# Layer 2 of a four-layer graph network on one Trainium2 core: counts in array quarters, ordered through POOL, and evicted by column chunk

## The chip, the core and the metric

The kernel runs on one core of a Trainium2 chip. The core has five engines that each take their own queue in order[...]: PE (TensorE, matrix products, with its weight loads shown apart as PEld), DVE (VectorE), ACT (ScalarE), POOL (GpSimd) and SP (which issues the DMAs here).[...] The metric is the device time of one execution in microseconds. The kernel before takes 688.06 us (median of 3 runs, 685.46 to 690.53).

## What is computed

Four graph layers follow each other on 3327 nodes with 64 features and one dense 3327 x 3327 adjacency matrix, each with a layer norm and a residual. The change concerns the third of them, which is called layer 2 in the code:

```python
support = input @ weight
mask = (adj != 0).astype(support.dtype)
rank = jnp.cumsum(mask, axis=1)
deg = rank[:, -1:]
k = jnp.minimum(deg, float(MAX_NEIGH))        # MAX_NEIGH = 100
pos = rank - (deg - k)
w = mask * jnp.where(pos > 0, DECAY ** (k - pos), 0.0)   # DECAY = 0.5
out = w @ support + bias
```

A neighbour's weight is a power of one half whose exponent is the number of neighbours that come after it in the row. So what is needed of every entry of the adjacency is a count: how many entries of its row further on are not zero.

## The kernel before

**Tiles.** The nodes are padded to 26 blocks of 128. The targets (the rows of the adjacency) are split in two groups, `GROUPS[0]` with 768 and `GROUPS[1]` with 896 targets in each of two halves h. A group's columns are cut in two chunks, `g.chunks`: 384 and 384 columns in group 0, 384 and 512 in group 1. I call group 1, which comes first, wide and group 0 narrow.

**Blocks.** `work` lists 52 pieces of work (i, c, a): group i, source chunk c from 12 down to 0, and a = 1 and then 0. Piece n covers 128 sources; two pieces, a = 1 and a = 0, make a pair and share two masks. `mask(n + 2)` makes the mask of the piece two further on: DVE compares an adjacency tile that SP's queue has loaded with zero and writes bf16. `stream` plans the loads.

**Counts.** `count(n, h)` (line 1657) multiplies masks by constant 128 x 64 triangles. The result of half h lies in `cnt[h]`, a PSUM tile of two banks; there counts go on accumulating from piece to piece, so each eviction reads a running total. Two source blocks s give the lower and the upper 64 partitions of the result, so that two matmuls with 64 weight columns each use the two halves of the array side by side. In the a = 1 pieces `rest_a` has its content in rows 0 to 63 and zeros in the other rows, and `tri_b` has its content in rows 64 to 127 and zeros in the others; both are applied with all 128 rows. `tri_a`, in the a = 0 pieces, fills all rows.

**Evictions.** `S.activation(w, e, AF.Relu, bias=ebias)` (line 1669) turns counts into 16-bit patterns that are read again as bf16 powers of two. That is ACT's work; the last three evictions with a = 0 and h = 1 are done by DVE (line 1667).

**Products.** `weigh(n, q)` (line 1681) multiplies the support, split into the three bf16 `parts`, by the weights `ws[n]` of column chunk q: six matmuls, accumulated in `acc2`. It trails the counts: `todo` holds (n, q) that wait, and `flush(n, most)` takes one or two of them after each `count` if they are at least `LAG` = 1 piece old and if the generator that makes their support has been issued.

**Order.** Engines run in the order of issue. Between counts, `weave.tick()` lets generators issue pieces of neighbouring stages: the end of layer 1 and the support at the beginning of layer 2 (`support`, up to some 318 us), and, once the wide group is finished, the node quantities of layer 3 (`nodes3`, lines 997 to 1144). The latter also issues the `xw<-xs` transfers on POOL's queue (lines 1049 and 1050). When the wide group is done, POOL clears the `pack` and `p2c` tiles (lines 1744 and 1745); in time this happens far earlier, since POOL has nothing else to do. After the last piece DVE makes two attention products of layer 3 (line 1290), clears accumulators (line 1758) and takes the sums of group 0 (`m_t`, line 640), from which the node chain of layer 3 goes on (line 537).

`gates` (line 752), in layer 0, is named by the prediction because it uses matmuls with 64 rows and 64 columns, a quarter of the array each:

```python
r = D * ((1 - h) ^ o)
product(out, h, (w_mh, w_hm)[h][:, 2, :], slice(r, r + D))
```

Of the kernel before, what the change touches and what calls it, by code (L numbers as in the profile page):

```python
# [8 lines left out]
F32 = mybir.dt.float32  # L9
BF16 = mybir.dt.bfloat16  # L10
# [8 lines left out]
D = 64  # L19
P = 128  # L20
NB = 26
# [52 lines left out]
GROUPS = [Group(0, 6), Group(6, HB)]  # L74
# [238 lines left out]
def gnn_kernel(ctx: ExitStack, tc: tile.TileContext, t, out):  # L313
    nc = tc.nc
    V, S, G, T = nc.vector, nc.scalar, nc.gpsimd, nc.tensor
# [13 lines left out]
    p0 = ctx.enter_context(left("p0"))  # L329
# [80 lines left out]
    weave = Weave()  # L410
# [11 lines left out]
    for i in range(2):  # L422
# [18 lines left out]
    tri_b, tri_a, rest_a, ones64 = (  # L441
        p0.tile([P, D], BF16, name=n) for n in ("tri_b", "tri_a", "rest_a", "ones64")
    )
    ebias, hg, lastf = (p0.tile([P, 1], F32, name=n) for n in ("ebias", "hg", "lastf"))
    last = p0.tile([P, 1], I32, name="last")

    scrap = p0.tile([P, 1], F32, name="scrap")
    pick = p0.tile([P, 8, 2], F32, name="pick")
    halves = p0.tile([P, 2], F32, name="halves")
    G.iota(last, pattern=[[0, 1]], base=0, channel_multiplier=1)  # L450
# [50 lines left out]
    def pair(i):  # L501

        return ps.tile([P, 1024], F32, name="pair", tag=f"pair{i}")
# [184 lines left out]
    edges = [nd.tile([P, 2 * g.w], BF16, name="edges", tag=f"edges{g.c0}") for g in GROUPS]  # L688
# [39 lines left out]
    for i, (ca, cb) in enumerate(starts):  # L728
        g = Group(ca, cb, part=i % 2)
# [130 lines left out]
    n = len(s_src) + len(f_src)  # L860
# [10 lines left out]
    n = len(LAYER1) - len(f_src)  # L871
# [12 lines left out]
    parts = [mb16[:, i * NB * D : (i + 1) * NB * D] for i in range(2)]  # L884
# [722 lines left out]
    with ExitStack() as c2:  # L1607
        mk = c2.enter_context(right("l2"))
        c2x = c2.enter_context(ExitStack())
        mkx = c2x.enter_context(right("l2x"))  # L1610
        WB, WL = 7, 3
        LAG = 1


        work = [(i, c, a) for i in (1, 0) for c in reversed(range(HB)) for a in (1, 0)]
        masks, ws, cnt, acc2, todo = {}, {}, {}, {}, []

        def mask(n):

            if n < len(work):  # L1620
                a = stream.tile(stream.now)
                w = 2 * GROUPS[work[n][0]].w
                masks[n] = (
                    spare if n == 4 else mk.tile([P, WIDE], BF16, name="mask", tag=f"mask{n % 5}")
                )
                V.tensor_scalar(masks[n][:, :w], a, 0.0, None, op0=OP.not_equal)  # L1626
                stream.done()

        def weights(n):
            b = n % (WB if n < NB else WL)  # L1630
            pool = mk if b < WL else mkx
            ws[n] = pool.tile([P, WIDE], U16, name="w", tag=f"w{b}")

        def count(n, h):

            i, c, a = work[n]
            g = GROUPS[i]
            first = n % NB == 0
            if h == 0 and n not in ws:
                weights(n)  # L1640
            if first:
                cnt[h] = pair(h)
            m = n - n % 2
            for lo, hi in g.chunks:
                cs = slice(h * g.w + lo, h * g.w + hi)
                terms = []
                if first:
                    terms.append([(ones64, edges[i][:, cs]), (tri_b, masks[m + 1][:, cs])])
                    terms.append([(tri_b, masks[m][:, cs])])
                elif a:  # L1650
                    terms.append([(rest_a, masks[m - 2 + s][:, cs]) for s in range(2)])
                    terms.append([(tri_b, masks[m + s][:, cs]) for s in range(2)])
                else:
                    terms.append([(tri_a, masks[m + s][:, cs]) for s in range(2)])
                for j, both in enumerate(terms):
                    for s, (l, r) in enumerate(both):
                        T.matmul(  # L1657
                            cnt[h][s * D : (s + 1) * D, P + lo : P + hi],
                            lhsT=l,
                            rhs=r,  # L1660
                            start=first and j == 0,
                            stop=j == len(terms) - 1 or first and s == 1,
                            skip_group_check=True,
                        )
            w, e = ws[n][:, h * g.w : (h + 1) * g.w], cnt[h][:, P : P + g.w]
            if gen_n and not weave.runs(gen_n) and a == 0 and h:
                V.tensor_scalar(w, e, ebias, 0.0, op0=OP.add, op1=OP.max)
            else:
                S.activation(w, e, AF.Relu, bias=ebias)  # L1669

        def weigh(n, q):
            i, c, a = work[n]
            g = GROUPS[i]
            if n % NB == 0 and q == 0:
                if i == 0:
                    weave.until(gen_s)
                acc2[i] = accumulators((0, 1) if i == 0 else (2, 3))
            lo, hi = g.chunks[q]
            for j, p in enumerate(parts):
                for h in range(2):  # L1680
                    T.matmul(  # L1681
                        acc2[i][q][h * D : (h + 1) * D, : hi - lo],
                        lhsT=p[:, 2 * c + a, :],
                        rhs=ws[n][:, h * g.w + lo : h * g.w + hi].bitcast(BF16),
                        start=n % NB == 0 and j == 0,
                        stop=n % NB == NB - 1 and j == 2,
                    )

        def flush(n, most):
            while todo and most and todo[0][0] <= n - LAG:  # L1690
                gens = need[work[todo[0][0]][1]]
                if weave.runs(*gens):
                    if len(todo) < 2 * WB:
                        return
                    weave.until(*gens)
                weigh(*todo.pop(0))
                most -= 1


        for n in range(WL):  # L1700
            weights(n)
        spare = mk.tile([P, WIDE], BF16, name="mask", tag="mask4")
        for n in range(2):
            mask(n)
        m_s = evicted(gs_, acc_s)
        gen_s = weave.add(support(gs_, m_s), 1, gen_f)
        need = {c: (gen_f if c >= gf.c0 else gen_s,) for c in range(HB)}
        gen_n = None
        for n in range(len(work)):
            mask(n + 2)  # L1710
            for part in range(2):
                count(n, part)
                flush(n, 2 if len(todo) > 2 * LAG + 2 else 1)
                todo.append((n, part))
                weave.tick()
            if gen_n or todo[0][0] < NB:
                continue

            m_f = evicted(gf, acc2[1], b_l2)
            turn["banks"] = (2, 3)  # L1720
            c2x.close()
            cc.close()
            stream.close(range(SLOTS2, SLOTS1))
            n3 = ctx.enter_context(left("n3"))
            h = n3.tile([P, NB, D], F32, name="h3")
            c3 = ctx.enter_context(ExitStack())
            n3f = c3.enter_context(left("n3f"))
            xd = n3f.tile([P, NB, D], F32, name="xd")

            xs = n3f.tile([P, HN], F32, name="xs")  # L1730
            xw = n3f.tile([P, HN], F32, name="xw")
            rows_j = n3f.tile([P, NP], BF16, name="rows_j")
            rows_i = n3f.tile([P, NP], BF16, name="rows_i")
            leftb = n3f.tile([P, NP], F32, name="leftb")
            p2c = n3f.tile([P, NB, 31 + ROWS], F32, name="p2c")
            x2, qs, pn, rpn, lefts, righth, B1, Bq2, alq, xq = (
                n3.tile([P, NB], F32, name=n)
                for n in "x2 qs pn rpn left righth B1 Bq2 alq xq".split()
            )
            least = n3.tile([P, 2], F32, name="least")  # L1740

            packs = [n3f.tile([P, GROUPS[1].nb, P], BF16, name=f"pack{i}") for i in range(2)]
            for a in packs:
                G.memset(a, 0.0)
            G.memset(p2c, 0.0)
            onesl = n3f.tile([12, P], BF16, name="onesl")
            V.tensor_scalar(onesl, last[:12, :].to_broadcast([12, P]), 9.0, None, op0=OP.is_ge)
            gen_n = weave.add(nodes3(gf, m_f))
            weave.add(early3(), 1, gen_n)
        flush(len(work) + LAG, len(todo))  # L1750
        while weave.running:
            weave.tick()
        for name, *args in (("attention_t", 0), ("attention_d", 0)):
            made3.add((0, name, *args))
            STEPS3[name](0, *args)
        x0, x1 = bank(2), bank(3)
        for a in (x0, x1):
            V.memset(a, 0.0)
        m_s = evicted(gs_, acc2[0], b_l2)
# [406 lines left out]
```

## Time and profile before

The profiled execution has a span of 680.8 us from its first to its last instruction; the median of the timed runs is 688.06 us.

| engine | busy us | share of the span | instructions |
|---|---|---|---|
| PE | 627.6 | 92% | 5656 |
| DVE | 457.4 | 67% | 725 |
| ACT | 391.2 | 57% | 561 |
| POOL | 9.3 | 1% | 19 |

Layer 2's own groups of instructions, from the page and from the answers by line:

| line | engine | what | count | median of one, ns |
|---|---|---|---|---|
| 1657 | PE | count matmuls `tri_b`, `tri_a`, `rest_a` | 208, 208, 192 | 326 |
| 1681 | PE | product matmuls | 624 | 326 |
| 1626 | DVE | masks | 52 | 1083 |
| 1669 | ACT | evictions | 101 | 992 |
| 1667 | DVE | evictions | 3 | 1018 |

Matmuls are pipelined, and a record also covers the way through the array: in a steady stream pairs of matmuls with 384 columns start every 0.16 us, although each record takes 0.33 us. How often the next one starts is what a matmul costs PE. The page's slices divide the span into 40 parts of 17 us; a digit is the busy share in tenths.

### The profile page before, as it was taken

The page shows a single profiled execution, that of the slowest core. Times are in us where ns is not written, and L with a number is a line of the kernel's source. Part 1 is how long each engine was busy: PE and PEld are TensorE (multiplying, and loading weights), DVE is VectorE, ACT ScalarE, POOL GpSimd, SP SyncE. Part 2 cuts the span into 40 slices and gives each one's busy share as a digit, 9 for nine tenths or more (in the row PEclk, how much of TensorE's full clock was granted, in tenths as well). Part 3 has the DMA queues.
Part 4 walks back from the last instruction along what each step waited for, and adds up shares of the span by engine and source line. Part 5 has one row for each costly group of instructions (what it writes and reads, how often), then busy time and mean ns, then how long its engine had stood idle before and what let it go on. Part 6 is the DMA issues. An engine that isn't in the chain of part 4 may idle for free.

```text
span 680.8 us, 13348 instructions
## 1 busy us (share of the span) xinstructions
PE 627.6 (92%) x5656; PEld 348.0 (51%) x5656; DVE 457.4 (67%) x725; ACT 391.2 (57%) x561; POOL 9.3 (1%) x19
## 2 busy tenths in 40 slices
PE   2988999999989999899998996799999999999993
PEld 1442444244334333466665663466666666676781
DVE  3331876544788705676558656699888889988875
ACT  3112200310354203588887788699899988988813
POOL 0000000000000000200001000100000000000000
PEclk9999999999999999999999999699999999999996
DMA  8999999099996999988787954157666666656401
GB/s 337 414 416 418 359 381 366 7 362 419 419 411 230 416 419 416 405 335 305 267 310 244 360 189 144 23 145 237 201 226 204 198 202 211 195 176 196 155 2 55
DMA packets 32531, 183.41 MB, mean 269 GB/s; under 512 B 3696, under 2 KB 4752, under 8 KB 32464
## 3 DMA queue, kind: packets, MB, share of 16 engines
q1 hardware_dynamic: 32112, 181.63, 72.2%
q0 software_dynamic: 352, 0.85, 0.5%
q8 instruction: 46, 0.75, 0.4%
q14 instruction: 21, 0.17, 0.1%
HBM read 180.76 MB, written 0.85 MB: 267 GB/s over the span
## 4 chain that ended last, share of the span: by engine, by line
PE 79%; DVE 8%; DMA 6%; ACT 5%; issue 1%; SPq 0%; DVEq 0%; ACTq 0%
PE bank L651 26%; PE bank L1330 17%; PE pair L1223 8%; PE pair L1657 7%; PE pair L1317 6%; PE bank L1681 6%; DMA adj<-in_adj 5%; PE pair L752 2%; ACT w L1669 2%; PE pair L556 1%; PE bank L1427 1%; DMA xn<-in_x 1%; PE bank L526 1%; PE bank L1057 1%; PE bank L1545 0%
## 5 line engine op out<-in xcount | busy, mean ns | idle before, releaser
L651 PE MATMUL bank<-adj,m_a 128*64 128x384 f32 (+1 forms) x832 | 153.8, 516 | 8.0 <-DMA adj<-in_adj 5.6
L651 PEld LDWEIGHTS bank<-adj,m_a 128*64 128x64 f32 x832 | 56.8, 137 | 94.6 <-issue 71.3
L1669 ACT ACTIVATE w<-pair,ebias 128x896 uint16<-128x896 f32 (+1 forms) x101 | 93.4, 954 | 17.2 <-PE pair L1657 16.0
L651 PE MATMUL bank<-adj,m_b 128*64 128x384 f32 (+1 forms) x416 | 76.7, 515 | 1.4 <-ACT hm L740 1.4
L1279 ACT ACTIVATE tr<-leftb,righth 128x256 f32<-128x256 f32 x156 | 66.4, 496 | 0.8 <-PE bank L1330 0.8
L1626 DVE TENSOR_SCALAR mask<-adj 128x1792 bf16<-128x1792 f32 (+1 forms) x52 | 52.8, 1034 | 18.8 <-PE pair L1657 18.8
L379 DVE SCALAR_TENSOR_TENSOR edges<-adj,edges 128x1792 bf16<-128x1792 f32 (+1 forms) x24 | 44.9, 1890 | 30.3 <-DMA adj<-in_adj 30.2
L1327 DVE SCALAR_TENSOR_TENSOR tr<-pair,tr 128x1024 f32<-128x1024 f32 (+3 forms) x52 | 49.7, 957 | 22.2 <-PE pair L1317 20.0
L1233 ACT ACTIVATE sq<-pair 128x1024 f32<-128x1024 f32 (+1 forms) x52 | 47.5, 912 | 22.6 <-PE pair L1223 21.7
L740 ACT ACTIVATE hm<-bank 64x384 f32<-64x384 f32 (+1 forms) x8 | 4.1, 513 | 93.1 <-DVE mh L739 92.8
L1681 PE MATMUL bank<-w,m_b 128*64 128x384 bf16 (+1 forms) x416 | 56.2, 339 | 0.0
L1223 PE MATMUL pair<-xs,xw 64*128 64x512 f32 (+3 forms) x120 | 54.7, 542 | 1.4 <-ACT sq L1233 1.4
L1223 PE MATMUL pair<-xs 64*128 64x512 f32 (+3 forms) x120 | 54.7, 542 | 1.2 <-ACT sq L1233 1.2
L1308 DVE SCALAR_TENSOR_TENSOR dir<-sq,dir 128x1792 f32<-128x1792 f32 (+2 forms) x27 | 52.5, 1946 | 0.0
L1290 DVE SCALAR_TENSOR_TENSOR dir<-dir,adj 128x1792 f32<-128x1792 f32 x26 | 52.4, 2016 | 0.0
L651 PEld LDWEIGHTS bank<-adj,m_b 128*64 128x64 f32 x416 | 29.0, 137 | 45.6 <-issue 41.9
L1256 ACT ACTIVATE dir<-leftb,righth 128x1792 f32<-128x1792 f32 (+6 forms) x38 | 48.5, 1307 | 0.0
L1243 ACT ACTIVATE sq<-sq,hg 128x1792 f32<-128x1792 f32 x26 | 46.6, 1791 | 0.8
L1317 PE MATMUL pair<-ident,sq 128*128 128x128 f32 x312 | 45.5, 282 | 0.1
L1290 DVE SCALAR_TENSOR_TENSOR tr<-tr,adj 128x1280 f32<-128x1280 f32 (+2 forms) x26 | 45.5, 1751 | 0.0
L1317 PEld LDWEIGHTS pair<-ident,sq 128*128 128x128 f32 x312 | 33.5, 142 | 22.2 <-issue 11.8
L1330 PE MATMUL bank<-dir,xd 128*64 128x384 f32 (+3 forms) x264 | 43.6, 460 | 0.0
(312 smaller groups left out, 948.2 us busy)
## 6 DMA issues: line engine op xcount, KB each, us to landing
adj<-in_adj SPq DMA_DIRECT2D x108, 896.0 KB, 6.3
adj<-in_adj SPq DMA_DIRECT2D x92, 768.0 KB, 8.2
adj<-in_adj SPq DMA_DIRECT2D x12, 640.0 KB, 4.0
xn<-in_x SPq DMA_DIRECT2D x3, 192.0 KB, 5.4
out<-w SPq DMA_DIRECT2D x3, 192.0 KB, 2.4
xw<-xs POOLq DMA_DIRECT2D x4, 128.0 KB, 4.0
w_l<-in_w_l SPq DMA_DIRECT2D x1, 460.0 KB, 9.8
xn<-in_x SPq DMA_DIRECT2D x1, 256.0 KB, 7.1
```

Of the source, the lines that this page charges most:

```text
L651: T.matmul(acc[q][h * D : (h + 1) * D, : hi - lo], lhsT=m[:, k, :], rhs=a[:, h * g.w + lo : h * g.w + hi], start=first, stop=last,)
L1223: T.matmul(p[:, o : o + n], lhsT=l, rhs=r, start=not rows, stop=rows)
L1256: S.activation(columns(dirs[m, b], ph.n)[:, :, first * P : first * P + n], left_of(ph.g)[:, :, o : o + n], AF.Tanh, bias=righth[:, 2 * c + ...
L1279: S.activation(a[:, e * 2 * P : (e + 1) * 2 * P].rearrange("p (b c) -> p b c", b=2), left_of(ph.s)[:, :, o : o + P], AF.Tanh, bias=righth[ ...
L1290: V.scalar_tensor_tensor(a[:, :w], a[:, :w], 1.0, stream.tile(stream.now), op0=OP.add, op1=OP.mult)
L1308: V.scalar_tensor_tensor(a[:, :, cs], s[:, :, cs], HD, a[:, :, cs], op0=OP.add, op1=OP.mult)
L1317: T.transpose(p[:, o : o + P], columns(sqs[m, b], PHASES[m].n)[:, k, i * P : (i + 1) * P], ident,)
L1327: V.scalar_tensor_tensor(a, pts.pop((m, k, "t"))[:, :n], HD, a, op0=OP.add, op1=OP.mult)
L1330: T.matmul(out, lhsT=lhsT, rhs=rhs, start=False, stop=True, skip_group_check=True)
L1626: V.tensor_scalar(masks[n][:, :w], a, 0.0, None, op0=OP.not_equal)
L1669: S.activation(w, e, AF.Relu, bias=ebias)
L1681: T.matmul(acc2[i][q][h * D : (h + 1) * D, : hi - lo], lhsT=p[:, 2 * c + a, :], rhs=ws[n][:, h * g.w + lo : h * g.w + hi].bitcast(BF16), s ...
```

## The change

`count` now takes a column chunk q in place of a half h, so `cnt[q]` holds both halves of one chunk, one in each bank, and `evict` reads 2 x 384 or 2 x 512 columns. Products are queued in pieces of two matmuls, (n, q, j) for the part j, and `flush`'s limits are three times as high. In a = 1 pieces that are not the first of their group, and for which a product piece can be issued, the counts are made by `count_rows` with matmuls of 64 rows and 64 columns, that is in quarters of the array. A first set of four for each chunk writes every region of the two banks once; a second set writes every region once more from the other half of the rows. Between the sets stand a POOL memset of one element, `seen`, which waits for the first set and for which the second set waits, and one product piece on PE. Evictions of chunk 1 in a = 1 pieces with even c are DVE's; the rule for the last three DVE evictions is gone.

```diff
+        def evict(n, q):
             i, c, a = work[n]
             g = GROUPS[i]
+            lo, hi = g.chunks[q]
+            w = ws[n][:, : 2 * g.w].rearrange("p (h c) -> p h c", h=2)[:, :, lo:hi]
+            e = cnt[q].rearrange("p (h c) -> p h c", h=2)[:, :, : hi - lo]
+            if a and q and c % 2 == 0:
                 V.tensor_scalar(w, e, ebias, 0.0, op0=OP.add, op1=OP.max)
             else:
                 S.activation(w, e, AF.Relu, bias=ebias)
...
+        def add_up(n, q, h, s, l, r, rs, start, stop):
+            g = GROUPS[work[n][0]]
+            lo, hi = g.chunks[q]
+            return T.matmul(
+                cnt[q][s * D : (s + 1) * D, h * 512 : h * 512 + hi - lo],
+                lhsT=l[rs],
+                rhs=r[rs, h * g.w + lo : h * g.w + hi],
+                start=start, stop=stop, skip_group_check=True,
+            )
...
+        def count_rows(n, q, second):
+            made = []
+            tiles = ((0, 0, 0), (0, 1, 1), (1, 1, 0), (1, 0, 1))
+            for h, s, upper in tiles[:: -1 if second else 1]:
+                if upper ^ second:
+                    l, r, rs = tri_b, masks[n + s], slice(D, P)
+                else:
+                    l, r, rs = rest_a, masks[n - 2 + s], slice(0, D)
+                made.append(add_up(n, q, h, s, l, r, rs, False, bool(second)))
+            return made
+
+        def ordered(later, earlier):
+            info = mybir.DependencyInfo(mybir.DependencyClass.Sync, mybir.DependencyReason.DATA)
+            tc.add_manual_dep(later.ins, earlier.ins.name, info, reason="row tiles")
...
             mask(n + 2)
-            for part in range(2):
-                count(n, part)
-                flush(n, 2 if len(todo) > 2 * LAG + 2 else 1)
-                todo.append((n, part))
-                weave.tick()
+            most = 6 if len(todo) > 6 * LAG + 6 else 3
+            if work[n][2] and n % NB and can_weigh(n):
+                weights(n)
+                for part in range(2):
+                    before = count_rows(n, part, 0)[-1]
+                passed = G.memset(seen, 0.0)
+                ordered(passed, before)
+                weigh(*todo.pop(0))
+                for part in range(2):
+                    ordered(count_rows(n, part, 1)[0], passed)
+                    evict(n, part)
+                flush(n, 2 * most - 1)
+                for part in range(2):
+                    pieces_of(n, part)
+                    weave.tick()
+            else:
+                for part in range(2):
+                    count(n, part)
+                    flush(n, most)
+                    pieces_of(n, part)
+                    weave.tick()
```

`can_weigh(n)` is true if the oldest piece in `todo` is at least one block old and its support has been issued; `pieces_of(n, part)` queues the three pieces of a chunk. Where counts are not made in quarters, `count` issues for each half the same matmuls as before, ordered by chunk.

More of the change, by code (lines that the diff above doesn't have):

```diff
@@ L447, in gnn_kernel @@
     scrap = p0.tile([P, 1], F32, name="scrap")
+    seen = p0.tile([1, 1], F32, name="seen")
     pick = p0.tile([P, 8, 2], F32, name="pick")
@@ L1632, in weights @@
             ws[n] = pool.tile([P, WIDE], U16, name="w", tag=f"w{b}")
-        def count(n, h):
+        def evict(n, q):
             i, c, a = work[n]
             g = GROUPS[i]
[L1638 to L1666, printed above, removed]
+            lo, hi = g.chunks[q]
+            w = ws[n][:, : 2 * g.w].rearrange("p (h c) -> p h c", h=2)[:, :, lo:hi]
+            e = cnt[q].rearrange("p (h c) -> p h c", h=2)[:, :, : hi - lo]
+            if a and q and c % 2 == 0:
                 V.tensor_scalar(w, e, ebias, 0.0, op0=OP.add, op1=OP.max)
@@ L1669, in count, with weigh @@
                 S.activation(w, e, AF.Relu, bias=ebias)
-        def weigh(n, q):
+        def add_up(n, q, h, s, l, r, rs, start, stop):
[5 more added lines that the diff above has]
+                rhs=r[rs, h * g.w + lo : h * g.w + hi],
+                start=start,
+                stop=stop,
+                skip_group_check=True,
+            )
+        def count(n, q):
+            i, c, a = work[n]
+            first = n % NB == 0
+            if n not in ws:
+                weights(n)
+            if first:
+                cnt[q] = pair(q)
+            m = n - n % 2
+            whole = slice(0, P)
+            for h in range(2):
+                if first:
+                    add_up(n, q, h, 0, ones64, edges[i], whole, True, False)
+                    add_up(n, q, h, 1, tri_b, masks[m + 1], whole, True, True)
+                    add_up(n, q, h, 0, tri_b, masks[m], whole, False, True)
+                    continue
+                if a:
+                    for s in range(2):
+                        add_up(n, q, h, s, rest_a, masks[m - 2 + s], whole, False, False)
+                for s in range(2):
+                    add_up(n, q, h, s, tri_b if a else tri_a, masks[m + s], whole, False, True)
+            evict(n, q)
+        def count_rows(n, q, second):
[11 more added lines that the diff above has]
+            tc.add_manual_dep(later.ins, earlier.ins.name, info, reason="row tiles")
+        def weigh(n, q, j):
             i, c, a = work[n]
             g = GROUPS[i]
-            if n % NB == 0 and q == 0:
+            if n % NB == 0 and q == j == 0:
                 if i == 0:
@@ L1678, in weigh, with can_weigh @@
             lo, hi = g.chunks[q]
[L1679 to L1687, printed above, removed]
+            for h in range(2):
+                T.matmul(
+                    acc2[i][q][h * D : (h + 1) * D, : hi - lo],
+                    lhsT=parts[j][:, 2 * c + a, :],
+                    rhs=ws[n][:, h * g.w + lo : h * g.w + hi].bitcast(BF16),
+                    start=n % NB == 0 and j == 0,
+                    stop=n % NB == NB - 1 and j == 2,
+                )
+        def can_weigh(n):
+            return todo and todo[0][0] <= n - LAG and not weave.runs(*need[work[todo[0][0]][1]])
         def flush(n, most):
@@ L1692, in flush @@
                 if weave.runs(*gens):
-                    if len(todo) < 2 * WB:
+                    if len(todo) < 6 * WB:
                         return
@@ L1697, in flush, with pieces_of @@
                 most -= 1
+        def pieces_of(n, part):
+            todo.extend((n, part, j) for j in range(3))
         for n in range(WL):
@@ L1710, in gnn_kernel @@
             mask(n + 2)
-            for part in range(2):
-                count(n, part)
-                flush(n, 2 if len(todo) > 2 * LAG + 2 else 1)
-                todo.append((n, part))
-                weave.tick()
+            most = 6 if len(todo) > 6 * LAG + 6 else 3
+            if work[n][2] and n % NB and can_weigh(n):
+                weights(n)
+                for part in range(2):
[16 more added lines that the diff above has]
+                    weave.tick()
             if gen_n or todo[0][0] < NB:
```

## The prediction

> **What bounds the kernel now.** I read the page's slices first, then busy time by stage, then the waits of the stage that the change touches. Layer 2 runs from about 280 us (first count, L1657) to 414 us (last product, L1681).
>
> ```profile
> PE   2988999999989999899998996799999999999993
> ACT  3112200310354203588887788699899988988813
> ```
> ```profile
> core 0: us, PE busy (x) PEld busy (x) DVE busy (x) ACT busy (x) POOL busy (x), PEclk, DMA share, GB/s
> 320.00:347.40 27.40, 27.40 (x306) 16.74 (x303) 15.78 (x18) 23.43 (x26) 0.00 (x0) 1.00 0.75 262
> 351.00:369.70 18.70, 15.62 (x168) 10.55 (x162) 16.99 (x32) 15.29 (x21) 0.26 (x1) 1.00 0.78 279
> 369.70:399.00 29.30, 29.30 (x336) 19.19 (x334) 17.84 (x44) 22.62 (x28) 1.95 (x4) 1.00 0.94 333
> 399.00:416.70 17.70, 16.05 (x177) 11.72 (x178) 9.67 (x10) 13.88 (x21) 0.00 (x0) 1.00 0.40 122
> ```
> PE never stops in rows one and three: PE time is elapsed time there. From 351 to 369.7 DVE is the full engine (16.99 of 18.70; the node chain of layer 3, with masks between). But ACT, which turns each count into a weight, is close behind PE (23.43 of 27.40). No mask in layer 2 waits for a DMA. Of the waits between 278 and 415 us, this pair matters:
>
> ```profile
> ACT w L1669 <- PE pair L1657: 16.0, 38, 1.6
> PE pair L1657 <- ACT w L1669: 5.9, 10, 2.0
> ```
> Counts accumulate on in one PSUM tile, so an eviction must be over before the next counts go into it. Today that costs PE 5.9 us in all, because between a count and the next one into the same tile lie another count and two products.
>
> **What the Trainium skill says.** *TensorEngine Tiling (Array Packing)*, Key Properties: tiles work independently, and changing the tiling mode, not just the tile, drains TensorE. The gates of layer 0 (L752) show both:
>
> ```profile
> 62.82 0.49 PE L752 MATMUL pair<-hm,w_l 128*64 128x384 f32 x1
> 62.83 0.95 PE L752 MATMUL pair<-mh,w_l 128*64 128x384 f32 x2
> 63.25 0.53 PE L752 MATMUL pair<-hm,w_l 64*64 64x384 f32 x1
> 63.25 0.53 PE L752 MATMUL pair<-mh,w_l 64*64 64x384 f32 x1
> 63.26 0.53 PE L752 MATMUL pair<-hm,w_l 64*64 64x384 f32 x1
> 63.61 0.48 PE L752 MATMUL pair<-mh,w_l 64*64 64x384 f32 x1
> ...
> 64.05 0.54 PE L651 MATMUL bank<-adj,m_a 128*64 128x384 f32 x2
> ```
> Pairs in half-arrays start 0.32 us apart. Quarters (64*64) start four at a time (63.24 to 63.26), but 0.42 after the last pair, and the halves return 0.41 after the last quarter (63.63 to 64.05): 0.10 us for each change of mode. First matmuls after it also take 0.53 instead of 0.49, a weight load laid bare. The same page, Gotcha 1, says that row tiles cannot use one PSUM bank at once; the L752 quarters do, on different partitions, and run together. *SBUF — State Buffer*, Reading the diagram: DVE's two-port operations and GpSimd share a port pair as an exclusive lock. The trace agrees: a mask beside a POOL memset took 1.41 us where 1.09 is usual.
>
> ```profile
> 284.34 0.92 POOL L1745 MEMSET p2c<- 128x988 f32 x1 [5.43 <-DVE mask L1626]
> 284.80 1.41 DVE L1626 TENSOR_SCALAR mask<-adj 128x1792 bf16<-128x1792 f32 x1
> ```
>
> **The parts, priced.** Streaming, by start-to-start times: a pair or quartet of 384 columns 0.16 us, of 512 columns 0.21; a record ends 0.17 after streaming, a semaphore takes 0.04. I count 0.12 per mode change (0.10, and 0.02 seen after L1139 at 399.1). Evictions:
>
> ```profile
> L1669 ACT ACTIVATE w<-pair,ebias 128x896 uint16<-128x896 f32 x52 | 50.4, 1005 | 6.4 <-PE pair L1657 5.6
> L1669 ACT ACTIVATE w<-pair,ebias 128x768 uint16<-128x768 f32 x49 | 42.9, 900 | 10.8 <-PE pair L1657 10.4
> L1667 DVE TENSOR_SCALAR w<-pair,ebias x3: 1018/1018/1018, 402.8 to 411.7; 128x768 uint16<-128x768 f32 x3
> ```
> Back to back on ACT the next one starts 0.11 before the end of the last (0.79 for 768). The chunk form makes 768 and 1024 columns out of 896 twice; for 1024 I extrapolate 1.11 on ACT, 1.29 on DVE.
>
> *PE work.* Of each pair of blocks (a=1, then a=0) the a=1 counts of both chunks stream 1.49 us in the wide group (group 1: four times 0.16 + 0.21), 1.28 in the narrow one (eight times 0.16). In quarters they halve: -0.75 and -0.64. Two sets with a product piece between them make four mode changes: +0.48. Net -0.27 and -0.16. This applies to 21 of 26 a=1 blocks (n = 8 to 24 and 28 to 50, even): in the compiled order POOL has 21 memsets of `seen`; the rest are group starts or have no product ready.
>
> *The POOL step.* From the end of streaming: record 0.17, POOL's start 0.06 (as at 284.34 after its mask), a one-column memset 0.10 (the four at the start of the program), back to PE 0.06: 0.39. The cover is change, product piece, change: 0.12 + 0.16 + 0.12 = 0.40. Nothing, if POOL answers so fast; any delay is paid whole, since PE takes its queue in order and set two, both evictions and all later products stand behind it.
>
> *The new wait.* Both chunks' set one now come directly after the a=0 block, so chunk 1 needs the eviction that has just begun. Narrow pair, times from PE's release into set one, chunk 1: set two starts at 0.56, its chunks end at 0.72 and 0.88; ACT evicts chunk 0 from 0.93 to 1.83; chunk 1 goes to ACT (1.72 to 2.62) or DVE (1.09 to 2.11). PE does five pieces until 1.80, waits until 1.87, counts a=0 chunk 0 until 2.19, three pieces, chunk 1 from 2.67 to 2.99. Its eviction runs on ACT from 3.30 to 4.20 (3.20 to 4.10 in a DVE pair). PE, after three pieces, a change and set one of chunk 0, is there at 3.75 and waits until 4.24 or 4.14. Mean period 4.19 against 3.84 by the same arithmetic before: **+0.35**. The wide pair in the same steps: 4.69 against 4.48 (4.54 measured): **+0.21**. The gain of 0.16 to 0.27 is lost to a stall of some 0.4 to 0.5.
>
> *DVE evictions.* Chunk 1 of a=1 goes to DVE where c is even: 14 of 104 evictions, for 3 today. In steady pairs they are in the periods above. On DVE each waits for set two, with the next mask and the node chain queued behind it. Between 351 and 369.7 DVE is the bound, so n=30 puts 1.02 straight into its chain; 0 if it falls where DVE waits, 2 with n=34. That stretch also swallows what PE gains or loses there (four pairs).
>
> *Tail.* Before, DVE holds the last eviction (411.69 to 412.71), then two layer-3 products of 1.4 and 2.0 us, two memsets, and the m_t eviction at 417.08. After, ACT has the last one: DVE starts its products earlier, but ACT carries one eviction more in a full stretch. I take -1 (from -3 to +1).
>
> *POOL's queue.* The pack and p2c memsets (4.1 us) now sit behind nine `seen`, but the next `seen` is four blocks (8 us) later: 0. The xw DMA issues (369.44 to 371.79, waiting for DVE's xs) stand before two `seen`: +0.3. A memset caught behind a mask waits up to 0.95 or 1.09; masks run right after set two, so mostly clear: +0.5 (0 to 5). SP's queue is not touched; its loads follow the masks.
>
> *Weight loads laid bare* after the two new waits, 0.05 each in 13 pairs: +1.3. Weigh pieces, write order and first blocks (n < 8): 0, from -1 (ACT is relieved near 288) to +2 (DVE was 9.6 of 10 us busy from 300 to 310); the cover is PE's backlog of products.
>
> Sum: wide n=10 to 24, 8 x 0.21 = 1.7; n=8, with a backlog of products and so no stall, -0.3; DVE stretch 1.0; n=36 to 44, 5 x 0.35 = 1.7; tail -1; 0.3 + 0.5 + 1.3. Total +5.2: the span goes from 680.8 to 686.0. The median shown, 688.06, lies 7.3 above that span (what is around the span, and run to run); so 693.3, **693 us**, +0.7%.
>
> **Rivals.**
> *Faster, the stall does not bite:* evictions in two runs of 384 finish nearer the 0.81 us that L1233 needs for its 768 columns, or other PE work fills the gap. Then 9 x 0.27 + 12 x 0.16 = 4.4 and 3 from the tail: 681. For it: before, PE hardly waits for ACT. Against: the release of set one, chunk 1 is a true dependency, one eviction after the last count. 0.18.
> *Slower, POOL answers late:* the place is set two; if the round trip takes 0.8 instead of 0.39 (a memset behind a mask's port lock, or slow to start), 0.4 x 17 pairs that PE bounds = 7: 700. It decides from 0.40 on. For it: the 1.41 us mask, and an xw issue beside a mask (369.44, 0.67 instead of 0.52). 0.22.
> *The quarters do not run together* in bf16, or two row tiles share a bank badly: each set takes twice as long, +0.7 x 17: 705. L752 speaks against it. 0.05.
> My forecast has 0.55, and runs by itself from 688 to 698.
>
> A measurement of this kernel tells about 1% from no change: below 681.2 or above 694.9. Faster: 0.10 from the first rival, 0.02 else. Slower: 0.38 of my own case (0.20), nearly all of the second and third: 0.44. Same: 0.44. The range leaves one in ten on each side: 684 to 702.
>
> **What would show it.** Right: PE waits of 0.3 to 0.5 us for the eviction at set one of chunk 1 in most pairs, periods near 4.7 and 4.2 us, quarters four at a time with 0.1 us on both sides, set two waiting for POOL under 0.1. Wrong: no such waits and periods near 4.2 and 3.7 (first rival), or a wait of several tenths for `seen` (second), or a shift mainly before 300 or after 400 us.

## The result, and the profile after

The kernel after takes **704.61 us** (median of 4 runs, 704.14 to 707.0); beside it the kernel before took 688.02 (4 runs, 685.46 to 690.53). The ratio is 1.0253, with a 95% interval from 1.0216 to 1.029: 14.9 to 20.0 us slower. The profiled execution of the kernel after has a span of 702.4 us.

First the page's slices of the kernel after, in tenths of a slice of 17.6 us; PEclk is the granted clock of TensorE.

```profile
PE   2988999999989998887986997599999999999994
ACT  3112200401545012666665578789989888898913
PEclk9999999999999999999998999799999999999997
```

Layer 2 is in the slices 17 to 25. PE's digits there were 8 9 9 9 9 8 9 9 6 and are 8 8 7 9 8 6 9 9 7; ACT's were 5 8 8 8 8 7 7 8 8 and are 6 6 6 6 6 5 5 7 8; and the clock dips in slice 22. So PE waits more, and not for an engine that is full. The windows of the kernel after say in which stretch of layer 2: the pieces n = 0 to 13, 14 to 25, 26 to 33, 34 to 45 and 46 to the last product. The columns are the length of the stretch and then the busy time of each engine.

```profile
core 0: us, PE busy (x) PEld busy (x) DVE busy (x) ACT busy (x) POOL busy (x), PEclk, DMA share, GB/s
282.25:330.30 48.05, 39.20 (x435) 21.52 (x431) 34.13 (x52) 31.35 (x40) 0.96 (x4) 0.96 0.77 282
330.30:358.81 28.51, 27.22 (x299) 14.78 (x296) 18.72 (x19) 19.62 (x23) 3.66 (x8) 1.00 0.69 249
358.81:387.09 28.28, 21.05 (x206) 11.22 (x202) 22.45 (x37) 17.01 (x22) 2.27 (x6) 0.88 0.74 250
387.09:418.04 30.95, 29.73 (x335) 15.93 (x334) 20.25 (x46) 19.65 (x25) 2.08 (x9) 1.00 0.85 281
418.04:434.60 16.56, 13.54 (x161) 8.25 (x162) 7.29 (x7) 13.19 (x19) 0.26 (x3) 1.00 0.42 128
```

Before, the same stretches took 39.48, 27.24, 22.20, 29.30 and 14.44 us. Layer 2 is 19.7 us longer in the profiled executions, 8.6 of it in the first stretch and 6.1 in the third. These are the two in which the end of layer 1 and the node chain of layer 3 are woven between the counts. The two steady stretches cost 1.3 and 1.7.

The waits from 278 to 440 us in the kernel after, where two stood before:

```profile
ACT w L1644 <- PE pair L1649: 38.3, 41, 2.5
DVE w L1642 <- PE pair L1649: 22.8, 11, 5.3
PE pair L1649 <- ACT w L1644: 15.0, 20, 3.2
PEld L1649 <- POOL seen L1749: 6.0, 21, 0.8
```

PE now waits 15.0 us for ACT's evictions (5.9 before) and 6.0 for POOL, and ACT and DVE wait longer for PE. Each waits for the other: a ring, not a bound.

A steady wide pair shows what the forecast described. These are matmuls of n = 18 and of the next a = 1 block, n = 20:

```profile
340.03 0.38 PE L1649 MATMUL pair<-mask,tri_b 64*64 64x512 bf16 x1
340.34 0.41 PE L1708 MATMUL bank<-w,m_b 128*64 128x512 bf16 x2
340.69 0.35 PE L1649 MATMUL pair<-mask,rest_a 64*64 64x384 bf16 x1
...
344.16 0.35 PE L1649 MATMUL pair<-mask,tri_b 64*64 64x384 bf16 x1
...
344.94 0.37 PE L1649 MATMUL pair<-mask,rest_a 64*64 64x512 bf16 x1 [0.43 <-ACT w L1644]
```

Set one, a product piece and set two follow each other at 0.31 and 0.35 us (0.21 of each is streaming, the rest the mode change and, before set two, POOL's answer). Set one of chunk 1 waits 0.43 for the eviction of the block before, which is still running.

The mixed stretches show something else. First n = 12, on PE and on ACT:

```profile
319.00 0.32 PE L1649 MATMUL pair<-mask,rest_a 64*64 64x384 bf16 x1 [0.97 <-ACT w L1644]
...
321.62 0.37 PE L1649 MATMUL pair<-mask,rest_a 64*64 64x512 bf16 x1 [2.26 <-ACT w L1644]
...
321.96 0.35 PE L1708 MATMUL bank<-w,m_b 128*64 128x384 bf16 x2
322.91 0.35 PE L1649 MATMUL pair<-mask,rest_a 64*64 64x384 bf16 x1 [0.59 <-POOL seen L1749]
...
323.41 0.53 PE L1708 MATMUL bank<-w,m_b 128*64 128x384 bf16 x2
```
```profile
317.31 0.84 ACT L602 ACTIVATE sq<-xc 128x768 f32<-128x768 f32 x1 [0.61 <-DVE xc L621]
318.06 0.88 ACT L1644 ACTIVATE w<-pair,ebias 128x768 uint16<-128x768 f32 x1
318.97 1.28 ACT L624 ACT_TABLE_LOAD   x1
320.26 0.30 ACT L624 ACTIVATE ln_var<-ln_var,eps 128x12 f32<-128x12 f32 x1
320.47 1.09 ACT L1644 ACTIVATE w<-pair,ebias 128x1024 uint16<-128x1024 f32 x1
```

The two evictions of n = 11 stand in ACT's queue among the layer norm of layer 1: the first behind line 602, which waits for DVE, the second behind the table load. Both chunks of set one need them, and PE has no product between the two. It waits 0.97 and 2.26, and then 0.59 for POOL, whose memset took 0.69 us instead of 0.09. After that the same product pair takes 0.53 where it took 0.35, because the granted clock has fallen. The windows around n = 12 and, in the last row, behind n = 32 show it in the column PEclk:

```profile
core 0: us, PE busy (x) PEld busy (x) DVE busy (x) ACT busy (x) POOL busy (x), PEclk, DMA share, GB/s
319.00:323.40 4.40, 1.54 (x18) 0.47 (x17) 2.33 (x4) 2.58 (x4) 0.69 (x1) 0.99 0.70 272
323.40:327.00 3.60, 3.60 (x22) 2.00 (x20) 1.66 (x2) 0.88 (x1) 0.00 (x0) 0.53 0.74 257
381.00:385.00 4.00, 4.00 (x26) 1.78 (x26) 2.44 (x9) 1.69 (x2) 0.09 (x1) 0.53 0.73 250
```

The place n = 32 is alike, here on ACT:

```profile
375.01 0.95 ACT L1013 ACTIVATE xc<-h_n 128x896 f32<-128x896 f32 x1 [1.56 <-DVE h_n L1010]
375.87 0.88 ACT L1644 ACTIVATE w<-pair,ebias 128x768 uint16<-128x768 f32 x1
...
378.04 1.28 ACT L990 ACT_TABLE_LOAD   x1
...
379.44 0.88 ACT L1644 ACTIVATE w<-pair,ebias 128x768 uint16<-128x768 f32 x1
```

PE waits 1.65 us for the first of these evictions, which stands behind a step of layer 3's chain that waits for DVE, and 3.19 for the second, behind the table load of line 990.

In the kernel after, DVE's timeline at n = 4 is:

```profile
290.40 2.09 DVE L1627 TENSOR_SCALAR mask<-adj 128x1792 bf16<-128x1792 f32 x2
294.41 1.28 DVE L1642 TENSOR_SCALAR w<-pair,ebias 128x1024 uint16<-128x1024 f32 x1 [1.92 <-PE pair L1649]
295.61 0.62 DVE L957 CAST m_b<-sq 128x896 bf16<-128x896 f32 x1
296.26 1.09 DVE L958 TENSOR_TENSOR h_t<-sq,m_b 128x896 bf16<-128x896 f32 x1
```

The new eviction waits 1.92 us for its count at the head of DVE's queue. Behind it stand lines 957 and 958, which make the `m_b` and `h_t` that PE's products need; PE waits 0.57 and 0.77 us for them.

### The profile page after: what moved, and what is told of

Same layout as the page of the kernel before. It is cut to its first block, busy times and chain, and to the rows that moved or that the text cites. A ratio compares the mean times of both kernels' runs of the same rounds, so it can differ in the third digit from the quotient of the medians.

```text
span 702.4 us, 13392 instructions
## 1 busy us (share of the span) xinstructions
PE 635.2 (90%) x5656; PEld 337.4 (48%) x5656; DVE 471.2 (67%) x736; ACT 381.2 (54%) x550; POOL 12.3 (2%) x40
## 4 chain that ended last, share of the span: by engine, by line
PE 71%; DVE 10%; ACT 9%; DMA 7%; issue 2%; SPq 0%; POOL 0%; DVEq 0%; ACTq 0%; POOLq 0%
PE bank L652 24%; PE bank L1331 17%; PE pair L1224 8%; DMA adj<-in_adj 6%; PE pair L1318 6%; PE bank L1708 5%; ACT w L1644 5%; PE pair L1649 4%; PE pair L753 2%; DVE mask L1627 1%; PE pair L557 1%; PE bank L1428 1%; DMA xn<-in_x 1%; PE bank L527 1%; PE bank L1058 1%
## 5 line engine op out<-in xcount | busy, mean ns | idle before, releaser
L1644 ACT ACTIVATE w<-pair,ebias 128x768 uint16<-128x768 f32 (+1 forms) x90 | 82.0, 943 | 41.0 <-PE pair L1649 38.3
L1708 PE MATMUL bank<-w,m_b 128*64 128x384 bf16 (+1 forms) x416 | 61.6, 351 | 0.6 <-DVE m_b L957 0.6
L1627 DVE TENSOR_SCALAR mask<-adj 128x1792 bf16<-128x1792 f32 (+1 forms) x52 | 54.3, 1065 | 5.8 <-PE pair L1649 5.8
L652 PEld LDWEIGHTS bank<-adj,m_b 128*64 128x64 f32 x416 | 28.9, 137 | 45.6 <-issue 41.0
L1649 PE MATMUL pair<-mask,rest_a 64*64 64x384 bf16 (+2 forms) x192 | 31.5, 354 | 15.3 <-ACT w L1644 14.2
L1318 PEld LDWEIGHTS pair<-ident,sq 128*128 128x128 f32 x312 | 34.0, 143 | 22.2 <-issue 11.8
```

Of the source, the lines that this page charges most:

```text
L652: T.matmul(acc[q][h * D : (h + 1) * D, : hi - lo], lhsT=m[:, k, :], rhs=a[:, h * g.w + lo : h * g.w + hi], start=first, stop=last,)
L1318: T.transpose(p[:, o : o + P], columns(sqs[m, b], PHASES[m].n)[:, k, i * P : (i + 1) * P], ident,)
L1649: return T.matmul(cnt[q][s * D : (s + 1) * D, h * 512 : h * 512 + hi - lo], lhsT=l[rs], rhs=r[rs, h * g.w + lo : h * g.w + hi], start=star ...
L1708: T.matmul(acc2[i][q][h * D : (h + 1) * D, : hi - lo], lhsT=parts[j][:, 2 * c + a, :], rhs=ws[n][:, h * g.w + lo : h * g.w + hi].bitcast(B ...
```

## The experiments

All are timed against the kernel before, which had medians of 688.06, 687.15 and 687.16 us in the three groups of runs. The theories: **lost slack** (both chunks' counts directly behind the a = 0 block hand ACT's delays to PE), **DVE evictions** (a wait for a count with a side chain queued behind it), **mode changes and quarters**, **late POOL**.

The table has the stretches of layer 2 in us, from the first count of one piece to that of another, at the end to the last product, and the median of the runs.

| kernel | 0-14 | 14-26 | 26-34 | 34-46 | 46-end | median |
|---|---|---|---|---|---|---|
| before | 39.5 | 27.2 | 22.2 | 29.3 | 14.4 | 688.0 |
| after | 48.1 | 28.5 | 28.3 | 31.0 | 16.6 | 704.6 |
| no_quarters | 45.4 | 28.2 | 24.5 | 29.3 | 14.8 | 695.8 |
| former_evictions | 44.3 | 28.5 | 27.5 | 30.7 | 15.2 | 701.4 |
| whole_rows | 48.5 | 32.7 | 29.1 | 33.1 | 18.2 | 715.1 |
| whole_rows_no_pool | 48.9 | 29.6 | 27.1 | 31.1 | 16.5 | 705.6 |
| chunks_only | 39.9 | 27.8 | 22.2 | 29.3 | 14.0 | 687.6 |
| before_adjacent | 40.2 | 27.9 | 24.8 | 29.5 | 14.5 | 692.1 |
| quarters_steady | 40.0 | 28.5 | 24.9 | 30.7 | 14.0 | 692.3 |
| dve_late | 39.9 | 28.2 | 24.4 | 29.3 | 14.8 | 690.0 |
| quarters_mixed_four | 43.1 | 27.8 | 26.0 | 29.3 | 14.0 | 695.2 |
| quarters_narrow | 39.9 | 27.8 | 22.2 | 32.1 | 14.0 | 690.9 |
| pieces_ahead | 40.4 | 28.9 | 24.1 | 29.8 | 14.0 | 694.4 |

### Parts taken out of the kernel after

**no_quarters**: all counts by `count`, chunks and DVE evictions kept.

```diff
-            if work[n][2] and n % NB and can_weigh(n):
+            if False:
```

> The changed kernel without quarters, POOL step and adjacent sets: a=1 pieces are counted by chunk with all rows, products between the chunks; DVE keeps its 14 evictions. Lost slack (both chunks' counts directly behind the a=0 piece hand every delay of ACT to PE): most of the 16.6 us comes back, 688 to 693. DVE evictions (each waits for counts with the side chain of layer 1 or 3 queued behind it): most of the loss stays, 698 or more.

**former_evictions**: only the division of the evictions goes back.

```diff
-            if a and q and c % 2 == 0:
+            if gen_n and not weave.runs(gen_n) and a == 0 and q:
```

> The changed kernel with the former rule of which evictions DVE makes (only the last a=0 ones of chunk 1). Lost slack: little changes, 700 to 705, since ACT then has 11 evictions more in the stretches where it already holds PE up. DVE evictions: 690 to 694, with the pairs n=4 and n=30 back at 5.6 and 5.1 us.

**whole_rows**: order and POOL step as after, but the matmuls of `count_rows` have all 128 rows, half of them zero in `rest_a` and `tri_b` (no mode change, twice the streaming). For this the sets are divided anew: the first holds all matmuls of `rest_a`, the second all of `tri_b`.

```diff
-            tiles = ((0, 0, 0), (0, 1, 1), (1, 1, 0), (1, 0, 1))
-            for h, s, upper in tiles[:: -1 if second else 1]:
-                if upper ^ second:
-                    l, r, rs = tri_b, masks[n + s], slice(D, P)
+            for h, s in ((0, 0), (0, 1), (1, 0), (1, 1)):
+                if second:
+                    l, r, rs = tri_b, masks[n + s], slice(0, P)
                 else:
-                    l, r, rs = rest_a, masks[n - 2 + s], slice(0, D)
+                    l, r, rs = rest_a, masks[n - 2 + s], slice(0, P)
```

> The changed kernel with the same order, the same POOL step and product piece, but the two sets made with all 128 rows: first all of rest_a, then all of tri_b. No change of mode, but twice the streaming in 21 pieces. Lost slack: stalls stay, and PE streams 0.75 or 0.64 us more and changes mode 0.5 us less in each: 703 to 710. Quarters and mode changes are to blame: 690 to 695.

**whole_rows_no_pool**: the same without the memset and its two waits.

> The same without the POOL step, which is not needed where all rows are used in order. Beside whole_rows this is the price of the POOL round trip in this order: lost slack says 0 to 3 us less, as the product piece covers most of it; a late POOL says 6 us less or more.

Measured: no_quarters 695.76 us (ratio 1.0118, 1.0087 to 1.0148), former_evictions 701.43 (1.0193, 1.0167 to 1.022), whole_rows 715.06 (1.039, 1.0367 to 1.0413), whole_rows_no_pool 705.62 (1.0247, 1.0222 to 1.0271). Read as steps: chunks, pieces and DVE evictions cost 7.7 us without any quarter; issuing both chunks' counts side by side in two sets 9.9 more; the POOL step another 9.4 (1.3 of it at n = 26, where quarters_narrow will tell why, and some 3.3 because five of the memsets took 0.31 to 1.01 us); and the quarters give 10.5 of that back. So neither the quarters nor their mode changes are the loss, which rules out the third theory. But quarters with the POOL step they need are only 1.0 us faster than whole rows without it. no_quarters fell between its two forecasts, former_evictions where lost slack had put it, whole_rows above its forecast, and 9.4 us for the POOL step is what a late POOL had been forecast to cost in that order; what POOL costs in the kernel after is read from its trace further down. The first two theories had to be separated.

### DVE evictions or chunks

**chunks_only**: no_quarters with the former division of the evictions too.

> Column chunks, queue pieces of two matmuls and pieces' limits as in the kernel after; counts as in the kernel before (no quarters, no POOL step, each chunk followed by its products), and the evictions divided as before (three on DVE). It differs from the run without quarters, 695.8 us, by the new DVE evictions alone. DVE-eviction theory (they wait for counts with the side chain queued behind them): at most 690, with the stretch of pieces 0 to 14 back from 45.4 to about 40 us. Chunk-order theory (the loss of 7.7 us comes from chunks and smaller product pieces): 693 to 697, the stretch unchanged.

Measured: 687.61 (1.0003, 0.9983 to 1.0022). Chunks and smaller pieces cost nothing. They only move six product matmuls from the last pair to n = 16 (30 for 24), so that 14 to 26 is 0.6 us longer and the end 0.4 shorter. The 8 us between this and no_quarters are the DVE evictions, and they lie in pieces 0 to 14 (39.9 against 45.4) and 26 to 34. In no_quarters, with no quarter to blame, DVE's timeline shows at n = 8 the same picture as at n = 4, and PE's what becomes of it:

```profile
304.63 2.09 DVE L1627 TENSOR_SCALAR mask<-adj 128x1792 bf16<-128x1792 f32 x2
309.33 1.28 DVE L1642 TENSOR_SCALAR w<-pair,ebias 128x1024 uint16<-128x1024 f32 x1 [2.60 <-PE pair L1649]
310.53 0.16 DVE L926 TENSOR_TENSOR th<-th,e 128x12 f32<-128x12 f32 x1
```
```profile
313.97 0.32 PE L1649 MATMUL pair<-mask,tri_b 128*64 128x384 bf16 x1 [1.74 <-DVE mask L1627]
```

DVE stands still for 2.60 us while the chain of layer 1 and the next masks are behind it; then PE waits 1.74 us for a mask.

**dve_late**: no_quarters with the new DVE evictions only from n = 14 on.

```diff
-            if a and q and c % 2 == 0:
+            if a and q and c % 2 == 0 and n >= 14:
```

> The run without quarters (695.8 us), with the new DVE evictions only from piece n = 14 on; those of n = 4, 8 and 12 are ACT's again. Queue theory (a DVE eviction waits at the head of DVE's queue for its count, and holds back the side chain and masks behind it while the end of layer 1 is woven in): 688 to 690, with pieces 0 to 14 taking about 40 us as in the kernel with chunks alone, and no wait of PE for a mask before piece 14. If each DVE eviction costs something anywhere: 693 to 695.

Measured: 690.03 (1.0044, 1.0027 to 1.0061), and 39.9 us for pieces 0 to 14. So four evictions (n = 0, 4, 8 and 12) cost 5.7 us. Most of the other 2.4 us is in the pair n = 32, which went from 7.65 to 10.15: at 362.15 DVE's eviction of n = 30 delays the node chain, ACT's table load comes later, and PE waits 2.41 instead of 1.96 us and then runs for 4.4 us at a clock that is 0.61 in the mean.

### Side by side, and where

**before_adjacent**: the kernel before with only the order of its counts changed.

```diff
+            if work[n][2] and n % NB and can_weigh(n):
+                for part in range(2):
+                    count(n, part)
+                flush(n, 2 * most)
...
```

> The kernel before, with one thing changed: in a = 1 blocks that have products ready the counts of both halves are issued side by side and the products behind them, as the change orders them; no chunks, no quarters, no POOL step. Lost-slack theory (this order puts the second count directly behind the eviction that has to be over, so that every delay on ACT stops PE): 696 to 698, the loss mostly in pieces 0 to 14 and 26 to 34, with PE's waits for ACT's evictions going from 5.9 to over 12 us. If the loss of 9.9 us for this order needs the chunks (evictions of 1024 columns): at most 690.

Measured: 692.05 (1.0065, 1.0042 to 1.0088), between the two forecasts. PE's waits for ACT rose to 8.8 us, not over 12. The order alone costs 5 us, half of it in 26 to 34, where the clock is at half for 3.4 us from 371.2. The rest of the 9.9 us needs the two sets, the chunks or DVE's evictions beside them; which of these was not tried.

**quarters_steady**: former evictions, and quarters only in n = 14 to 24 and 34 to 44.

```diff
-            if work[n][2] and n % NB and can_weigh(n):
+            if work[n][2] and (14 <= n < 26 or 34 <= n < 46) and can_weigh(n):
```

> The kernel after, with evictions divided as before and with quarters (two sets, POOL step) only in the pieces n = 14 to 24 and 34 to 44, where no chain of a neighbouring layer is woven in. Lost-slack theory with a share for the mixed stretches: the steady stretches keep their +1.3 and +1.7 us, the others return to what chunks alone give; 690 to 693, and 701.4 less this is what the quarters' order costs in mixed stretches, about 9. If the loss is spread over all pairs: 697 or more.

Measured: 692.29 (1.0079, 1.0053 to 1.0104). Ten blocks fewer in quarters (21 before, 11 now) give back 9.1 of the 13.8 us between chunks_only and former_evictions. The steady stretches keep their cost (0.7 and 1.4 more than chunks_only). But 26 to 34 is at 24.9, not at 22.2, although no block in it is in quarters.

**quarters_mixed_four**: as quarters_steady, with `n in (10, 12, 30, 32)`.

> Chunks and pieces as in the kernel after, evictions divided as before (687.6 us), and quarters with the POOL step in four blocks only, n = 10, 12, 30 and 32, which are the ones beside side chains where the kernel after loses most. Lost-slack theory with ACT's side work as the cause: 692 to 695, over 1 us for each of the four, most of it at n = 12 and 32. If a quarter block costs the same wherever it is (0.4 us, as in the steady stretches): 689 to 690.

Measured: 695.16 (1.0114, 1.0095 to 1.0133). Four blocks cost nearly as much as all the new DVE evictions alone. By pairs it is 2.8 us at n = 12, 2.8 at 32, 0.9 at 30 and 0.2 at 10: the two with a table load in ACT's queue, not all four as I expected. In both the clock then falls, so part of the 2.8 us is the clock's. The table load and the chain around it were not tried apart.

**quarters_narrow**: as quarters_steady, with `34 <= n < 46` alone.

> As the run with quarters in the steady stretches (692.3 us), but only in n = 34 to 44. POOL-queue theory (the clearing of pack and p2c, 4.1 us on POOL, stands behind the last seen of the wide group and so falls on DVE's masks of n = 26 and 27; without those seen it runs at about 285 us as before): pieces 26 to 34 return from 24.9 to 22.2 us, 34 to 46 stay at 30.7, the time is 688.5 to 689.5. If pieces 26 to 34 stay near 25 us, it is not POOL's queue: 691 to 692.

Measured: 690.86 (1.0051, 1.0024 to 1.0078), more than expected, but pieces 26 to 34 are back at 22.20 us. POOL's and DVE's timelines of quarters_steady show why they were not:

```profile
347.04 0.09 POOL L1749 MEMSET seen<- 1x1 f32 x1 [4.85 <-PE pair L1649]
347.31 3.13 POOL L1793 MEMSET pack<- 128x1792 bf16 x2 [0.17 <-issue]
350.36 0.93 POOL L1794 MEMSET p2c<- 128x988 f32 x1
```
```profile
347.79 6.05 DVE L1627 TENSOR_SCALAR mask<-adj 128x1536 bf16<-128x1536 f32 x3 [2.97 <-PE pair L1649]
```

and DVE's timeline of quarters_narrow:

```profile
347.86 1.83 DVE L1627 TENSOR_SCALAR mask<-adj 128x1536 bf16<-128x1536 f32 x2 [2.58 <-PE pair L1649]
349.97 0.96 DVE L1627 TENSOR_SCALAR mask<-adj 128x1536 bf16<-128x1536 f32 x1 [0.28 <-PE pair L1649]
```

The clearing of `pack` and `p2c` is stuck behind the last `seen` of the wide group and runs when it is done, right beside three masks: 6.05 us for them instead of 2.79. PE then waits 1.3 us for a mask at the start of the narrow group, and the pair n = 26 takes 5.44 us instead of 3.94; in the kernel after it takes 5.81. That is 1.5 of the 2.7 us of quarters_steady. The other 1.2 are at n = 32 (8.89 for 7.65), and are not a longer wait: PE waits 0.63 and 1.95 us for ACT there, as in chunks_only and in quarters_narrow, but in quarters_steady the clock was at half from 369.73 to 373.14. In quarters_narrow the cost came elsewhere: n = 36 took 5.69 us, for 4.38 in quarters_steady, with a clock of 0.51 from 379.2 to 382.6 us. That is why its stretch 34 to 46 missed the 30.7 that I expected.

**pieces_ahead**: quarters_steady with two product pieces moved ahead of set one.

```diff
                 weights(n)
+                flush(n, 2)
...
-                flush(n, 2 * most - 1)
+                flush(n, 2 * most - 3)
```

> The run with quarters in the steady stretches, with two of the five product pieces behind set two put ahead of set one, so that the eviction that chunk 1 waits for has 0.32 to 0.43 us more. If the stall of the steady blocks comes from too little work between the a = 0 counts and set one: 689.5 to 690.5, and periods of 4.4 and 3.9 us. If it is a closed ring (set one, POOL, set two, two evictions, the a = 0 count, its eviction, set one again), which takes about 4.75 and 4.3 us whatever stands where: unchanged, 691.5 to 693, with the wait moved from set one to the a = 0 counts.

Measured: 694.43 (1.0116, 1.0083 to 1.015), against 692.29, and above both forecasts. In the wide group the pairs n = 20 and 22 stay at exactly 4.94 us, and n = 18, which waited for nothing before, now takes 4.75 us for 4.32: a closed ring. In the narrow group n = 38 and 40 get some 0.3 us shorter (5.29 for 5.62, 5.02 for 5.34), as too little work in between would have it. Layer 2 is 0.9 us shorter in the trace, and the time isn't; the intervals overlap, and where the 2 us would be stays open.

**before_last_on_act**: the kernel before, its very last eviction on ACT.

```diff
-            if gen_n and not weave.runs(gen_n) and a == 0 and h:
+            if gen_n and not weave.runs(gen_n) and a == 0 and h and n + 1 < len(work):
```

> The kernel before, with only its very last eviction moved from DVE to ACT, so that DVE begins layer 3's products about 1 us earlier. Forecast tail term (-1): 686.5 to 687.5. If ACT, full at the end, only delays PE's last products: 688 to 689.

Measured: 686.55 (1.0000, 0.9986 to 1.0015): no difference, and no kernel here beats the one before. DVE starts its attention products at 410.17, 5.5 us before the last product starts (before: 0.9), but the next step (`xn`, line 997) comes 4.6 us after that product, for 4.8 before:

```profile
416.49 0.48 DVE L1774 MEMSET bank<- 128x512 f32 x1 [0.18 <-DVE m_t L640]
420.29 0.69 DVE L997 TENSOR_TENSOR xn<-xn,bank 128x512 f32<-128x512 f32 x1 [3.31 <-PE bank L537]
```

DVE is early and waits 3.31 us for a transpose that stands in PE's queue behind line 1223.

## Why the prediction was wrong

The time got longer, to which I had given 0.44, no more than to no change. The mechanism that I priced is there in the steady blocks. The size was wrong, 5 us for 16.6, outside the range, because I carried the price of the steady blocks to blocks that are not steady, and put the new DVE evictions at their own duration. The 705 of my third rival meets the number, but not for its reason: the quarters do run together.

**Right.** Narrow: five times 0.35 = 1.75 for n = 36 to 44, measured 1.63. At n = 36 to 42 chunk 1's first quarters start 0.58 to 0.63 us after chunk 0's, for 0.19 where nothing is waited for (n = 34): a stall of some 0.4, as forecast. Wide: six times 0.21 = 1.26 for n = 14 to 24, measured 1.27, but by luck. Quarters are in n = 6 to 14 and 18 to 24 (POOL's timeline); n = 14 and 18 gain 0.25 and 0.22 us, and n = 20 to 24 lose 0.36, 0.40 and 0.27, which makes 0.56. The other 0.71 is at n = 16, which has no quarters; 0.56 of it are the six product matmuls that chunks_only has there too. The gain at n = 14 and 18 is the net -0.27 that I had for a block without a stall: n = 18 follows a block without quarters, and the ring isn't closed yet. The stall at n = 20 to 24 is longer than the 0.4 to 0.5 that I had: chunk 1 starts 0.79 us after chunk 0 for 0.19, some 0.6, of which the profile counts 0.43 as idle.

Quarters run four at a time, and a change of mode costs about 0.1 us. That changed modes drain TensorE is what the Trainium skill's *TensorEngine Tiling (Array Packing)*, Key Properties, says; it gives no price. POOL was to answer in 0.39 us: the record's 0.17, then 0.13 to the memset, 0.09 for it and 0.05 back, are 0.44. In 20 of the 21 blocks set two starts 0.05 us after the memset's end, so POOL's answer, and not the mode change, sets its start. Beyond the product piece's streaming and 0.10 for the change, that is 0.03 to 0.09 us in 17 blocks, and 0.20, 0.38 and 0.69 in the three whose memset was slow (0.21, 0.39 and 0.69 us): some 2.4 us in all, an estimate. So the rival of a late POOL did not decide, but it cost more than the 0.5 of my sum.

**Wrong, by size:**

1. *"Weigh pieces, write order and first blocks (n < 8): 0"*, and under *DVE evictions*, *"each waits for set two, with the next mask and the node chain queued behind it"*, which I then priced at 1.02 for n = 30 alone. Those at n = 0, 4, 8 and 12 cost 5.7 us (dve_late against no_quarters). I had written down the queue and charged the instruction's own duration, not the wait in front of it: 1.92 us at n = 4 in the kernel after, 2.60 at n = 8 in no_quarters.
2. *"wide n=10 to 24, 8 x 0.21 = 1.7"*, and *"That stretch also swallows what PE gains or loses there"* of the DVE stretch. At n = 12, 30 and 32 the block in quarters cost 2.8, 0.9 and 2.8 us (quarters_mixed_four), for 0.21 at n = 12 and nothing at n = 30 and 32 in my sum. The ring needs ACT's eviction at once, and ACT's queue holds a table load and a chain that itself waits for DVE. A stretch in which another engine is the bound does not swallow a delay if that engine's chain runs through PE, as here: DVE's `xn` (line 998) takes what PE has transposed (line 538), and waits 1.89 us for it at 358.45 in chunks_only.
3. *"The pack and p2c memsets (4.1 us) now sit behind nine `seen`, but the next `seen` is four blocks (8 us) later: 0."* I asked who waits behind them on POOL's queue, and not whom they shut out where they now run. It is the lock that *SBUF — State Buffer*, Reading the diagram, describes, and that I had shown at 284 us: 1.9 us at n = 26 in the kernel after, 1.5 in quarters_steady. quarters_narrow, whose clearing runs earlier, brings it back to nothing.
4. *The tail, -1.* The stretch 46 to the end is 2.1 us longer, and after it `xn` gains 0.2. It is no steady stretch either: PE waits 0.83 us at n = 48 and 0.56 and 1.47 at n = 50 for evictions that stand in ACT's queue behind layer 3's activations (lines 1257 and 1280). before_last_on_act shows that DVE's early start is given away to PE's queue.
5. *Not in the sum at all*: after PE's long waits its clock falls. In the kernel after 3.6 us from 323.4 and 4.0 us from 381 ran at 0.53; at full speed they would take 1.9 and 2.1, so some 3.6 us of the loss is this: an estimate, which takes PE there as bound by its clock alone. It lies within the losses at n = 12 and 32, not beside them. *TensorE: Matmul & The Clock Gate*, HAM oscillation, says that an idle gap of more than about 3.4 us halves the clock. The trace agrees in the halving, but not in the gap: no wait at n = 12 was longer than 2.26 us, with PE busy 1.54 of 4.40 us, and at n = 32 the clock fell at 377.97, when only 0.8 us of the wait of 3.19 had passed.

The parts do not simply add: at n = 32 DVE's eviction alone gives 10.15 us, the quarters alone 10.44, and both together 10.29. That is one reason why the DVE rule, which costs 8.2 us alone, costs only 3.2 on top of the quarters. One misreading was smaller: the profiled span of the kernel before was 7.3 us under its median, those of the other kernels lay between 0.6 over and 4.1 under theirs, so the 19.7 us of the two traces overstate the 16.6 that was timed.

## What to carry to other kernels

Price a tighter dependency in the busiest place that it reaches, not in the steady one: look up there what else stands in the queue of the engine that must answer, table loads above all, and charge the wait ahead of a moved instruction to everything behind it. A small instruction that makes a lazy queue wait also moves that queue's old work; find out beside whom it will now run. And stalls of 2 to 3 us on PE can cost more than themselves: at n = 12 and 32 the clock came back 3.9 and 4.4 us after PE did.

## What was not expected of the hardware

- The granted clock fell to one half without a long gap. In every kernel's trace it changes only at instants that lie a multiple of 3.41 us apart. In the kernel after it is at half from 323.35 to 326.76 and from 377.97 to 384.79 us; in the 3.41 us ahead PE was busy for 1.14 and 0.97 us. The kernel before and quarters_steady have the same waits at n = 32, but the steps lie differently: before, PE was busy 1.45 us of the step from 362.26, and the clock stayed; in quarters_steady it was busy 1.33 us of the step from 366.32, and the clock was at half for the next. Between the first and the last count of the 14 traces a full clock fell after all 14 steps in which PE was busy for up to 0.42 of the time, and after one of the others, which all have 0.43 or more. That one is in quarters_narrow at 379.12, with PE busy for 0.94; ahead of it lie 14 matmuls with only four columns each (line 1058). What sets it off there was not tried.
- A one-element POOL memset takes 0.09 us, but 0.69 beside a DVE mask (n = 12), where it ends 0.03 us after the mask, and up to 1.01 in whole_rows.
- Quarters on different partitions of one PSUM bank start within 10 ns of each other in the steady blocks and run together in bf16, as in f32 at line 752 (within 20 ns).
